# Grouped attention logits computed once and kept in SBUF, with GpSimd subtracting their maximum

## The chip, the cores and the metric

The kernel runs on one core of one Trainium2 chip. The time is the device time in microseconds of one execution. Five engines matter here: TensorE (PE) multiplies matrices into PSUM, VectorE (DVE), ScalarE (ACT) and GpSimd (POOL) work elementwise, and SyncE (SP) issues most of the loads. PSUM has eight banks of 128 partitions x 512 fp32; GpSimd has no operand in PSUM in this kernel.

## The reference, cut to what matters

Four cross-attention layers in fp32 run one after the other on x (4 batches, 512 queries, 256 channels) against one context (4 batches, 1024 keys, 512 channels). Layers 0, 2 and 3 are masked: 16 heads of 64.

```python
logits = einsum('bhqd,bhkd->bhqk', q, k) * scale + col_bias   # col_bias: a few key columns get -20*(1-mask)
probs  = softmax(logits)
out    = einsum('bhqk,bhkd->bhqd', probs, v) @ Wo + bo + residual
```

Layer 1 is grouped: an RMS norm of x, 16 query heads of 16 that share 4 key and value heads, no bias column, no `bo`:

```python
xn     = rmsnorm(x) * norm_w
scores = einsum('btgrd,bsgd->bgrts', qg, k) / 4      # 4 groups g, 4 query heads r in each
out    = einsum('bgrts,bsgd->btgrd', softmax(scores), v) @ wo + residual
```

## The kernel before

**Units and steps.** A unit (`Group`) is two masked heads of one layer and batch, or, in layer 1, the two kv groups of a half `h` (0 or 1) with one query head `r`. Logits are stored as keys x queries: block `t` of a unit is one tile of 128 keys by 2 x 512 queries, eight blocks in a unit, kept in slots `st[ring][t]` of SBUF. Two rings exist, each with eight blocks and a ninth slot (`mx`, also used as `acc`).

There are 96 masked units and 32 grouped ones. `order()` writes out 96 steps; each has one masked unit `g`, and 32 of them also have one grouped unit `lam`. The grouped units stand in four blocks of eight steps, one block for each batch. In step n, `g1` is the masked unit of step n-1, and `coming` is the grouped unit of step n+1. All engines execute the order in which the Python code issues the instructions (a manual schedule), and a semaphore holds an instruction back until its inputs and its output place are free.

**PSUM places.** `Place(width)` takes one or two banks, and always the ones that were given back longest ago, when the program is written; `back()` gives them back, and `late=` makes them look younger than they are. Which bank an instruction writes is therefore fixed in the program, and the matrix engine waits if the last reader of that bank has not finished.

**A masked unit.** `scores(g)`: eight pairs of matmuls into PSUM, ACT copies every block to SBUF (L674), DVE keeps a running maximum in the place of block 0 (L678). `max_quarters` (L715, L723, L747) and `max_everywhere` (L754) reduce it over the keys and spread it. DVE subtracts it (L759), ACT takes exponentials (L765), GpSimd adds the blocks (`running_sum`, L804) into `acc`. One step later `attend(g1)` (L694) multiplies with the values, `reciprocal_sums` (L820 to L834) and `scale_out` (L845) normalise, and after that `project_out` (L863) projects two units at a time and DVE adds the result to the state (L885).

**A grouped unit before.** Its heads have 16 dimensions in strips of 32 rows, so four matmuls run side by side in the array: `logits_pair(g, i)` (L643) makes two blocks at once. It is called twice for each unit. In step n-1 `maxima_pair` makes the logits for the maximum alone: DVE takes the maximum directly from PSUM (L635), and nothing is stored. `lower_queries` then writes minus the maximum into the query tile, into row 16 of every strip, where the keys hold a one (the bias `row16` in `k_grouped`, L503). In step n `exponentials_pair` makes the logits again, now already lowered, and ACT takes the exponentials from PSUM into SBUF (L651). The step's order on the matrix engine is: `scores(g)`, then four times two blocks of `attend(g1)` and one `logits_pair` of `lam`, then the fill.

**The fill.** After that come the rest of a step's matmuls, each 1.7 to 3.6 us in a planner's clock `now`: `project_out`, `project_q`, then keys of the next two units (L478, after odd masked units) or values (L519, after even ones), with the pairs of `coming` between them, and `attend(lam)`. DVE's subtractions and ACT's exponentials are issued between them by `events`, a list with due times in the same clock. A step in this text is called keys step or values step by its fill.

Of the kernel before, what the change touches and what calls it, by code (L numbers as in the profile page):

```python
# [28 lines left out]

# [48 lines left out]
def kernel(ctx: ExitStack, tc: tile.TileContext, a: dict, out: bass.AP):  # L78
# [18 lines left out]
    class Place:  # L97
        def __init__(self, width=2):
            free = given_back
            if width == 2:  # L100
# [19 lines left out]
    def st_slot(n):  # L120
# [11 lines left out]

    row16 = t_([P, 2], "row16", "row16")
    nc.vector.reduce_sum(
        row16[:, 0:1], ident.rearrange("p (g d) -> p g d", d=32)[:, :, 16], axis=AX.X
    )
    nc.vector.tensor_scalar(row16[:, 1:2], row16[:, 0:1], -1.0, None, ALU.mult)

# [346 lines left out]
    def k_grouped(g, h, part):  # L485

        if h == 0 and part == 0:
            g.kts = [t_([P, T // 2], f"kt1{i}", f"kt1{i}_{g.name}") for i in range(2)]
            g.kt = g.kts[0]
        if part == 0:  # L490
            g.k_place = Place(1)
        w = g.k_place
        m = w.ap
        for k in (2 * part, 2 * part + 1):
            for odd in range(2):
                nc.tensor.matmul(  # L496
                    m[64 * odd : 64 * (odd + 1), :], lhsT=g.w["k"][:, k, 64 * h : 64 * (h + 1)],
                    rhs=ctx_t[g.b][:, k, :].rearrange("p (i e q) -> p e i q", e=2, q=P)[:, odd],
                    start=(k == 0), stop=(k == KT - 1),
                )  # L500
        if part:
            return lambda: (
                nc.scalar.activation(g.kts[h], m, AF.Identity, bias=row16[:, 0:1]), w.back()  # L503
            )
# [124 lines left out]
    def maxima_pair(g, i):  # L629

        for odd, w in enumerate(logits_pair(g, i)):
            if i == 0 and odd == 0:
                nc.scalar.copy(g.mx, w.ap)  # L633
            else:
                nc.vector.tensor_tensor(g.mx, g.mx, w.ap, ALU.max)  # L635
            w.back()

    def logits_pair(g, i):
        ws = [Place(), Place()]
        for odd in range(2):  # L640
            for j in range(2):
                rows = slice(64 * odd + 32 * j, 64 * odd + 32 * (j + 1))
                nc.tensor.matmul(  # L643
                    ws[odd].ap[:, j * S : (j + 1) * S], lhsT=g.kt[rows, i * P : (i + 1) * P],
                    rhs=g.qt[rows, :], start=True, stop=True,
                )
        return ws

    def exponentials_pair(g, i):
        for odd, w in enumerate(logits_pair(g, i)):  # L650
            nc.scalar.activation(g.st[2 * i + odd], w.ap, AF.Exp)  # L651
            w.back()

    def scores(g):
# [3 lines left out]
        for t in range(NT):  # L658
# [16 lines left out]
            if t:  # L675
                w.back()
                top = g.mx_place.ap
                nc.vector.tensor_tensor(top, top, g.st[t], ALU.max)  # L678

    def place_out(g, width=1):  # L680
        g.place = Place(width)
        g.po, g.psum = g.place.ap[:, 0:S], g.place.ap[:, S:]
# [23 lines left out]
    def keep_odd(g):  # L706
        half = gq[g.b, "o"][64 * g.h : 64 * (g.h + 1), :]
        nc.vector.tensor_tensor(half, half, g.po[64:128, :], ALU.add)
        g.place.back()
# [16 lines left out]
    def lower_queries(g):  # L726


        half = max_halves(g, g.mx)
        every = t_([P, S // 32, 1], "every1", f"every1_{g.name}")  # L730
        for c in range(4):
            cols = slice(c % 2 * S // 32, (c % 2 + 1) * S // 32)
            nc.vector.tensor_tensor(
                every[32 * c : 32 * (c + 1), :, 0], half[0:32, cols], half[32:64, cols], ALU.max
            )

        m = g.mx[:, 0:S]
        nc.vector.transpose(
            m.rearrange("p (b r) -> p b r", r=32), every.to_broadcast([P, S // 32, 32])
        )  # L740
        nc.vector.scalar_tensor_tensor(g.qt, m, row16[:, 1:2], g.qt, ALU.mult, ALU.add)

# [8 lines left out]
    def max_everywhere(g):  # L751
        g.mb_place = Place()
        g.mb = g.mb_place.ap
# [4 lines left out]
    def subtract(g, t):  # L758
        nc.vector.tensor_tensor(g.st[t], g.st[t], g.mb, ALU.subtract)  # L759
        if t == NT - 1:  # L760
            g.mb_place.back()
# [82 lines left out]
    def scale_out(g):  # L844
        nc.vector.tensor_tensor(g.ot, g.po, g.ot, ALU.mult)  # L845
        g.place.back()

    def project_out(*of):
# [23 lines left out]
        def add():  # L872
# [13 lines left out]
            w.back()  # L886
# [56 lines left out]
    for b in range(B):  # L943
        first = next(g for g in masked if (g.b, g.l, g.u) == (b, 0, 0))
        for n, part_of in enumerate(load_parts(b, first.n == 0)):
            at_step = -1
            if first.n:
                before = masked[first.n - 2]
                at_step = step_of[before.l, before.b, before.u] - 5 + n
# [40 lines left out]
    turned = []  # L990
    left = {b: 32 - 4 for b in range(B)}

    for n in range(len(steps) + 2):
# [46 lines left out]
        pairs = []  # L1040
# [10 lines left out]
        def pair(i):  # L1051
            if i == 0:
                behind_exponentials()
            maxima_pair(coming, i)
            if i == NT // 2 - 1:
                lower_queries(coming)

        if coming:
            share(coming)
            coming.mx = st_slot((NT + 1) * (count % 2) + NT)  # L1060
        if lam:

            lam.st = [st_slot((NT + 1) * ((count if g else count + 1) % 2) + t) for t in range(NT)]
# [7 lines left out]


        if g:
            g.now = NT if masked_at(g.n + 1) else 4
            scores(g)

        ending = n >= len(steps) - 2
        if g1 and (g or lam):
            place_out(g1, 2 if ending else 1)
        if g:  # L1080
            max_quarters(g)
            if not lam:
                g.mx_place.back()
                max_everywhere(g)
        if turned or lam and g1:

            w = Place(1)
            if lam and g1:
                reciprocal_sums(g1, w.ap)
            for each in turned:  # L1090
                normalise_grouped(each, w.ap)
            w.back(late=12 if turned else 0)
        turned.clear()
        if lam:
            for i in range(NT // 2):
                if g1:
                    attend(g1, range(2 * i, 2 * i + 2))
                if coming and not g:
                    pair(i)
                exponentials_pair(lam, i)  # L1100
                if i == 0 and g:
                    g.mx_place.back()
                if not g:
                    if i == 1 and outs:
                        project_out(*outs.pop(0))()
                    if i == 2 and queries:
                        project_q(queries.pop(0))()
            if g and queries:


                project_q(queries.pop(0))()
            if g1:
                scale_out(g1)
                ready.append(g1)
            if g:
                max_everywhere(g)
        elif g1 and g:
# [3 lines left out]
        elif g1:  # L1121
            attend_last(g1)
            adds = [project_out(*each) for each in outs]
            outs = []
# [9 lines left out]
        if coming and (g or not lam):  # L1134
            pairs += [((12.0 if lam else 11.0 if g else 0.0) + 2.5 * i, i) for i in range(NT // 2)]

        fill, of_grouped = (
            [
                (1.8 * len(each), lambda each=each: project_out(*each))
                for each in outs if lam or each[0].masked == m
            ]
            for m in (True, False)
        )
        if lam:
            of_grouped = []
        outs = []  # L1150
        of_queries = [(1.7, lambda each=each: project_q(each)) for each in queries]
        fill += of_queries
        if lam:

            def attend_grouped():
                lam.v = head(lam).v
                place_out(lam)
                attend(lam)
                return lambda: keep_even(lam)

            fill.append((3.6, attend_grouped))
            late.append(lambda: keep_odd(lam))
# [18 lines left out]
        if follows and follows.l and follows.u == 0:  # L1181

            fill[-1:-1] = [(1.7, lambda: project_q(follows))]
        if g1 and g and ending:
# [9 lines left out]
        for us, w in fill:  # L1194
            while pairs and pairs[0][0] <= now:
                pair(pairs.pop(0)[1])
                now += 1.0
                pairs = [(max(at, now + 1.6), i) for at, i in pairs]
# [5 lines left out]
        while pairs:  # L1204
            pair(pairs.pop(0)[1])
# [36 lines left out]
```

## Time and profile before

| | |
|---|---|
| median of 3 runs | 3692.93 us (3689.32 to 3693.71) |
| the profiled execution | 3692.11 us; its span 3690.3 us |
| busy, share of the span | PE 99%, DVE 80%, ACT 57%, POOL 44% |
| granted TensorE clock | 0.999 |
| the four blocks of eight steps with a grouped unit, from one `scores` to the `scores` after the block | 372.74, 372.37, 372.34, 373.11 us |

The spans of the blocks are differences of the start times of the bias matmuls (L670) of their first steps. Durations in the profile are those of one execution; instructions of one engine overlap by their pipeline, so the distance from start to start can be a little shorter than a duration (ACT copies: 1051 ns each, eight in 7.43 us) or longer where each needs the one before (DVE maxima: 1233 ns each, seven in 9.25 us).

### The profile page before, as it was taken

Reading aid. Unit: us, or ns where it says so; the run is one execution under the profiler, and the core shown is the slowest. Engines: PE = TensorE matmul, PEld = TensorE weight load, DVE = VectorE, ACT = ScalarE, POOL = GpSimd, SP = SyncE. Lnnn points to the kernel's source line nnn. Section 1 sums busy time; section 2 is a strip of 40 time slices with the busy share of each in tenths; the row PEclk is TensorE's granted clock in tenths of the full one; section 3 lists DMA queues with packets and bytes.
Section 4 is the critical chain, followed back from the end, with each engine's and each line's share of the span. In section 5 each row is a group of like instructions: output and inputs, shape, how many; then the busy total and the mean of one; then the engine's idle time right before and its main releaser. Section 6 shows DMA issues by size and latency. Waiting matters only on the chain.

```text
span 3690.3 us, 42021 instructions
## 1 busy us (share of the span) xinstructions
PE 3656.6 (99%) x15534; PEld 1709.0 (46%) x15534; DVE 2970.3 (80%) x3912; ACT 2112.2 (57%) x2433; POOL 1622.7 (44%) x749
## 2 busy tenths in 40 slices
PE   8999999999999999999999999999999999999999
PEld 4554444444444444444545445454444445454454
DVE  7777788877888778887888778887788878888787
ACT  4555565555555656556555555555565565555554
POOL 3555433333333333333554545555333334545454
PEclk9999999999999999999999999999999999999999
DMA  2101100000000000000000110000100010000100
GB/s 65 43 32 40 34 28 22 21 21 23 22 22 21 21 23 22 22 22 18 26 18 26 49 38 26 26 26 18 33 22 22 13 33 18 26 26 26 32 28 9
DMA packets 137681, 98.16 MB, mean 27 GB/s; under 512 B 41720, under 2 KB 133368, under 8 KB 137476
## 3 DMA queue, kind: packets, MB, share of 16 engines
q1 hardware_dynamic: 131822, 82.37, 7.6%
q0 software_dynamic: 2560, 8.39, 0.8%
q10 hardware_dynamic: 3094, 4.72, 0.5%
q8 instruction: 122, 2.00, 0.2%
q14 instruction: 83, 0.68, 0.1%
HBM read 89.16 MB, written 2.10 MB: 25 GB/s over the span
## 4 chain that ended last, share of the span: by engine, by line
PE 94%; DVE 3%; ACT 1%; issue 1%; DMA 0%; POOL 0%; ACTq 0%; DVEq 0%; POOLq 0%
PE ps L694 21%; PE ps L519 18%; PE ps L478 18%; PE ps L664 17%; PE ps L643 8%; PE ps L863 5%; PE ps L575 5%; DVE ps L678 1%; DVE st L759 1%; PE ps L542 1%; PE ps L496 1%; PE ps L670 1%; ACT st L651 0%; PE ps L374 0%; ACT st L674 0%
## 5 line engine op out<-in xcount | busy, mean ns | idle before, releaser
L804 POOL TENSOR_TENSOR st<-st 128x1024 f32<-128x1024 f32 x668 | 1578.9, 2364 | 2014.0 <-ACT st L765 1969.2
L678 DVE TENSOR_TENSOR ps<-ps,st 128x1024 f32<-128x1024 f32 x672 | 828.4, 1233 | 430.4 <-ACT st L674 368.5
L765 ACT ACTIVATE st<-st 128x1024 f32<-128x1024 f32 x768 | 782.2, 1054 | 424.5 <-DVE st L759 412.6
L759 DVE TENSOR_TENSOR st<-st,ps 128x1024 f32<-128x1024 f32 x768 | 881.7, 1213 | 3.2
L694 PE MATMUL ps<-st,v 128*64 128x512 f32 (+1 forms) x4064 | 810.9, 598 | 0.0
L674 ACT COPY st<-ps 128x1024 f32<-128x1024 f32 x768 | 713.8, 1051 | 64.2 <-PE ps L670 63.0
L664 PE MATMUL ps<-qt,kt 64*128 64x512 f32 x3072 | 703.3, 597 | 0.9 <-ACT st L674 0.7
L478 PE MATMUL ps<-ctx,wk 128*128 128x512 f32 x1536 | 691.6, 601 | 2.2 <-ACT ctx L380 2.2
L519 PE MATMUL ps<-wv,ctx 128*128 128x256 f32 x3072 | 690.3, 382 | 0.0
L519 PEld LDWEIGHTS ps<-wv,ctx 128*128 128x128 f32 x3072 | 577.1, 190 | 152.5 <-issue 57.3
L694 PEld LDWEIGHTS ps<-st,v 128*64 128x64 f32 (+1 forms) x4064 | 231.2, 130 | 551.5 <-issue 467.4
L478 PEld LDWEIGHTS ps<-ctx,wk 128*128 128x128 f32 x1536 | 286.5, 191 | 395.3 <-issue 368.0
L664 PEld LDWEIGHTS ps<-qt,kt 64*128 64x128 f32 x3072 | 283.9, 186 | 358.0 <-ACT st L674 164.4
L635 DVE TENSOR_TENSOR st<-st,ps 128x1024 f32<-128x1024 f32 x224 | 273.5, 1221 | 151.8 <-ACT st L633 91.3
L651 ACT ACTIVATE st<-ps 128x1024 f32<-128x1024 f32 x256 | 248.1, 1021 | 154.7 <-PE ps L643 124.1
L643 PE MATMUL ps<-qt,kt 32*128 32x512 f32 x2048 | 305.4, 640 | 4.9 <-DVE st L759 3.4
L483 ACT COPY kt<-ps 128x512 f32<-128x512 f32 x192 | 111.4, 580 | 318.2 <-PE ps L478 318.0
L526 ACT COPY v<-ps 128x512 f32<-128x512 f32 x192 | 111.6, 583 | 248.2 <-PE ps L519 247.5
L581 ACT ACTIVATE qt<-ps 128x512 f32<-128x512 f32 x96 | 57.0, 594 | 269.1 <-PE ps L575 269.1
L575 PE MATMUL ps<-x,wq 128*128 128x512 f32 x384 | 188.8, 614 | 1.7 <-ACT x L352 1.1
L863 PE MATMUL ps<-ot,wo 128*128 128x512 f32 x384 | 176.5, 602 | 4.2 <-ACT st L651 3.5
L643 PEld LDWEIGHTS ps<-qt,kt 32*128 32x128 f32 x2048 | 90.2, 183 | 182.5 <-ACT st L651 51.9
(147 smaller groups left out, 1630.8 us busy)
## 6 DMA issues: line engine op xcount, KB each, us to landing
wk<-in_L_xattn_Wk_dram SPq DMA_DIRECT2D x47, 512.0 KB, 3.5
wv<-in_L_xattn_Wv_dram SPq DMA_DIRECT2D x47, 512.0 KB, 3.6
wq<-in_L_xattn_Wq_dram SPq DMA_DIRECT2D x96, 128.0 KB, 3.5
wo<-in_L_xattn_Wo_dram SPq DMA_DIRECT2D x96, 128.0 KB, 3.3
qt<-qt ACTq DMA_DIRECT2D x32, 128.0 KB, 2.2
xraw<-in_x_dram SPq DMA_DIRECT2D x3, 512.0 KB, 4.1
out_dram<-out SPq DMA_DIRECT2D x3, 512.0 KB, 3.7
wq<-in_L_xattn_wq_dram SPq DMA_DIRECT2D x32, 32.0 KB, 2.4
```

Source lines behind the costliest of these rows:

```text
L478: nc.tensor.matmul(m, lhsT=g.w["k"][:, k, :], rhs=ctx_t[g.b][:, k, n * 512 : (n + 1) * 512], start=(k == 0), stop=(k == KT - 1),)
L519: nc.tensor.matmul(m[:, half * 2 * P : (half + 1) * 2 * P], lhsT=ctx_t[g.b][:, k, t * P : (t + 1) * P], rhs=g.w["v2"][:, k, :], start=(k = ...
L575: nc.tensor.matmul(m, lhsT=g.wq[:, k, :], rhs=x[:, k, :], start=(k == 0), stop=(k == KC - 1))
L643: nc.tensor.matmul(ws[odd].ap[:, j * S : (j + 1) * S], lhsT=g.kt[rows, i * P : (i + 1) * P], rhs=g.qt[rows, :], start=True, stop=True,)
L664: nc.tensor.matmul(m[:, j * S : (j + 1) * S], lhsT=g.kt[g.rows[j], keys], rhs=g.qt[g.rows[j], :], start=True, stop=t > 0,)
L674: nc.scalar.copy(g.st[t], m)
L678: nc.vector.tensor_tensor(top, top, g.st[t], ALU.max)
L694: nc.tensor.matmul(g.po[at, :], lhsT=g.v[:, t, rows], rhs=g.st[t][:, j * S : (j + 1) * S], start=(t == first), stop=(t == last),)
L759: nc.vector.tensor_tensor(g.st[t], g.st[t], g.mb, ALU.subtract)
L765: nc.scalar.activation(st, st, AF.Exp)
L804: nc.gpsimd.tensor_tensor(g.acc, g.st[0] if t == 1 else g.acc, g.st[t], ALU.add)
L863: nc.tensor.matmul(m[:, k * S : (k + 1) * S], lhsT=each.wo[:, k * P : (k + 1) * P], rhs=each.ot, start=each is g, stop=each is of[-1],)
```

## The change

The logits of a grouped unit are made once, in its own step. `grouped_pair` makes two blocks, ACT copies both to SBUF, and DVE keeps a running maximum, as for a masked unit. The maximum is reduced and spread into a tile in SBUF (`mb`), GpSimd subtracts it from the eight blocks (`subtract_grouped`), and ACT takes the exponentials in place. `maxima_pair`, `lower_queries` and the row of ones are gone.

The order of a step with a grouped unit changes with it. First come the four rounds of `attend(g1)` and `grouped_pair(lam)`, then DVE's work for `lam` and `g1` (maximum, reciprocal sums, scaling, normalising of a grouped pair), the projections of queries, and only then `scores(g)`. The exponentials of `g`'s blocks 4 to 7 are not issued in their own step but carried into the next, two behind each `grouped_pair`. `attend(lam)` becomes the last item of the fill. Several `back(late=)` calls shift the choice of banks, and the context transposes of batches 0 and 2 are due two steps earlier.

```diff
-    def maxima_pair(g, i):
-        for odd, w in enumerate(logits_pair(g, i)):
-            if i == 0 and odd == 0:
-                nc.scalar.copy(g.mx, w.ap)
-            else:
-                nc.vector.tensor_tensor(g.mx, g.mx, w.ap, ALU.max)
-            w.back()
-    def exponentials_pair(g, i):
-        for odd, w in enumerate(logits_pair(g, i)):
-            nc.scalar.activation(g.st[2 * i + odd], w.ap, AF.Exp)
-            w.back()
+    def grouped_pair(g, i):
+        if i == 0:
+            g.mx_place = Place()
+        for odd in range(2):
...
+        for t in (2 * i, 2 * i + 1):
+            w = g.places[t]
+            nc.scalar.copy(g.st[t], w.ap)
+            if t:
+                w.back()
+                nc.vector.tensor_tensor(g.mx_place.ap, g.mx_place.ap, g.st[t], ALU.max)
+    def subtract_grouped(g, t):
+        nc.gpsimd.tensor_tensor(g.st[t], g.st[t], g.mb, ALU.subtract)
...
+        if lam:
+            share(lam)
+            lam.st = [st_slot((NT + 1) * (count % 2) + t) for t in range(NT)]
...
+            for i in range(NT // 2):
+                attend(g1, range(2 * i, 2 * i + 2))
+                grouped_pair(lam, i)
+                pass_carried(2)
+            max_quarters(lam)
+            lam.mx_place.back(late=5)
+            max_everywhere(lam)
+            for t in range(NT):
+                subtract_grouped(lam, t)
+            w = Place(1)
+            reciprocal_sums(g1, w.ap)
+            scale_out(g1)
+            for each in turned:
+                normalise_grouped(each, w.ap)
+            w.back(late=12)
...
+            run(of_queries)
...
         if g:
             g.now = NT if masked_at(g.n + 1) else 4
-            scores(g)
+            scores(g, pass_carried)
+        pass_carried(NT)
...
+        if lam:
+            for t in range(NT):
+                events.append((-3.0 + 2.36 * t, lambda t=t: nc.scalar.activation(lam.st[t], lam.st[t], AF.Exp)))
         if g:
             for t in range(NT):
-                events.append((0.7 + 1.2 * t, lambda t=t: subtract(g, t)))
-                events.append((3.3 + 1.22 * t, lambda t=t: exponentials(g, t)))
+                events.append(
+                    (3.7 + 0.01 * t if lam else 0.7 + 1.2 * t, lambda t=t: subtract(g, t, behind))
+                )
+                exp = lambda g=g, t=t: exponentials(g, t)
+                if not lam:
+                    events.append((3.3 + 1.22 * t, exp))
+                elif t < 4:
+                    events.append((14.5 + 1.22 * t, exp))
+                else:
+                    carried.append(exp)
```

More of the change, by code (lines that the diff above doesn't have):

```diff
@@ L97, with __init__ @@
     class Place:
-        def __init__(self, width=2):
+        def __init__(self, width=2, beside=None):
             free = given_back
-            if width == 2:
+            if beside and beside.banks[0] ^ 1 in free:
+                at = beside.banks[0] ^ 1
+            elif width == 2:
                 at = min(
@@ L131 @@
     nc.vector.memset(eps, EPS)
[L133 to L137, printed above, removed]
     def one_row(j):
@@ L501, in k_grouped @@
         if part:
-            return lambda: (
-                nc.scalar.activation(g.kts[h], m, AF.Identity, bias=row16[:, 0:1]), w.back()
-            )
+            return lambda: (nc.scalar.copy(g.kts[h], m), w.back())
     def v_pair(g, n, half):
@@ L626, in rms_norm @@
         return evacuate
[L629 to L639 removed]
+    def grouped_pair(g, i):
+        if i == 0:
+            g.mx_place = Place()
         for odd in range(2):
+            t = 2 * i + odd
+            w = Place() if t else g.mx_place
             for j in range(2):
@@ L643, in logits_pair, with scores @@
                 nc.tensor.matmul(
-                    ws[odd].ap[:, j * S : (j + 1) * S], lhsT=g.kt[rows, i * P : (i + 1) * P],
+                    w.ap[:, j * S : (j + 1) * S], lhsT=g.kt[rows, i * P : (i + 1) * P],
                     rhs=g.qt[rows, :], start=True, stop=True,
                 )
-        return ws
-    def exponentials_pair(g, i):
-        for odd, w in enumerate(logits_pair(g, i)):
-            nc.scalar.activation(g.st[2 * i + odd], w.ap, AF.Exp)
-            w.back()
-    def scores(g):
+            g.places.append(w)
+        for t in (2 * i, 2 * i + 1):
[6 more added lines that the diff above has]
+        nc.gpsimd.tensor_tensor(g.st[t], g.st[t], g.mb, ALU.subtract)
+    def scores(g, between):
         g.st = [st_slot((NT + 1) * g.ring + t) for t in range(NT)]
@@ L678, in scores, with place_out @@
                 nc.vector.tensor_tensor(top, top, g.st[t], ALU.max)
-    def place_out(g, width=1):
-        g.place = Place(width)
+            between()
+    def place_out(g, width=1, beside=None):
+        g.place = Place(width, beside)
         g.po, g.psum = g.place.ap[:, 0:S], g.place.ap[:, S:]
@@ L708, in keep_odd @@
         nc.vector.tensor_tensor(half, half, g.po[64:128, :], ALU.add)
-        g.place.back()
+        g.place.back(late=8)
     def over_quarter(out_, of, op):
@@ L724, in max_halves @@
         return half
[L726 to L741, printed above, removed]
     def max_quarters(g):
@@ L751, in max_everywhere @@
     def max_everywhere(g):
-        g.mb_place = Place()
-        g.mb = g.mb_place.ap
+        if g.masked:
+            g.mb_place = Place()
+            g.mb = g.mb_place.ap
+        else:
+            g.mb = t_([P, 2 * S], "stage", f"mb_{g.name}")
         nc.vector.transpose(
@@ L756, in max_everywhere, with subtract @@
         )
-    def subtract(g, t):
+    def subtract(g, t, late=0):
         nc.vector.tensor_tensor(g.st[t], g.st[t], g.mb, ALU.subtract)
         if t == NT - 1:
-            g.mb_place.back()
+            g.mb_place.back(late)
     def exponentials(g, t):
@@ L845, in scale_out, with project_out @@
         nc.vector.tensor_tensor(g.ot, g.po, g.ot, ALU.mult)
-        g.place.back()
-    def project_out(*of):
+        g.place.back(late=6)
+    def project_out(*of, late=0):
         g = of[0]
@@ L885, in add @@
                 nc.vector.tensor_tensor(acc, y, x if opens else acc, ALU.add)
-            w.back()
+            w.back(late)
         left[g.b] -= len(of)
@@ L948 @@
                 before = masked[first.n - 2]
-                at_step = step_of[before.l, before.b, before.u] - 5 + n
+                at_step = step_of[before.l, before.b, before.u] - (5 if b in (1, 3) else 7) + n
             parts.setdefault(at_step, []).append(part_of)
@@ L990 @@
     turned = []
+    carried = []
     left = {b: 32 - 4 for b in range(B)}
@@ L1039 @@
         late = []
-        pairs = []
         def pass_events(us):
@@ L1049, in behind_exponentials, with pass_carried @@
                 late.pop(0)()
[L1051 to L1063, printed above, removed]
+        def pass_carried(count=1):
+            for _ in range(count):
+                if carried:
+                    carried.pop(0)()
         queries = []
@@ L1070 @@
                 queries.append(each)
+        behind = 8 if lam else 0
+        of_outs = [
+            (1.8 * len(each), each[0].masked, lambda each=each: project_out(*each, late=behind))
+            for each in outs
+        ]
+        of_queries = [(1.7, lambda each=each: project_q(each)) for each in queries]
+        of_grouped = [(us, w) for us, of_masked, w in of_outs if not of_masked]
+        fill = [(us, w) for us, of_masked, w in of_outs if of_masked]
+        ending = n >= len(steps) - 2
+        if lam:
+            share(lam)
+            lam.st = [st_slot((NT + 1) * (count % 2) + t) for t in range(NT)]
+            lam.places = []
+            before = at(n - 1)[1]
+            place_out(g1, beside=before.place if before else None)
+            for i in range(NT // 2):
[13 more added lines that the diff above has]
+            w.back(late=12)
+            turned.clear()
+            ready.append(g1)
+            run(of_queries)
+            fill += of_grouped
+            of_queries = of_grouped = []
         if g:
             g.now = NT if masked_at(g.n + 1) else 4
-            scores(g)
-        ending = n >= len(steps) - 2
-        if g1 and (g or lam):
+            scores(g, pass_carried)
+        pass_carried(NT)
+        if g1 and g and not lam:
             place_out(g1, 2 if ending else 1)
@@ L1081 @@
             max_quarters(g)
[L1082 to L1085, printed above, removed]
+            g.mx_place.back()
+            max_everywhere(g)
+        if turned:
             w = Place(1)
-            if lam and g1:
-                reciprocal_sums(g1, w.ap)
             for each in turned:
                 normalise_grouped(each, w.ap)
[L1092 to L1117, printed above, removed]
+            w.back(late=12)
+            turned.clear()
+        fill += of_queries
+        if g1 and g and not lam:
             attend(g1)
@@ L1120 @@
                 late.append(lambda: normalise(g1))
-        elif g1:
+        elif g1 and not g:
             attend_last(g1)
-            adds = [project_out(*each) for each in outs]
-            outs = []
+            adds = [w() for _, w in fill + of_grouped]
+            fill, of_grouped = [], []
             reciprocal_rows(g1.ot, g1.psum, g1.mx)
@@ L1128 @@
                 add()
+        if lam:
+            for t in range(NT):
+                events.append((-3.0 + 2.36 * t, lambda t=t: nc.scalar.activation(lam.st[t], lam.st[t], AF.Exp)))
         if g:
             for t in range(NT):
-                events.append((0.7 + 1.2 * t, lambda t=t: subtract(g, t)))
-                events.append((3.3 + 1.22 * t, lambda t=t: exponentials(g, t)))
-            events.sort(key=lambda e: e[0])
[L1134 to L1162, printed above, removed]
+                events.append(
[6 more added lines that the diff above has]
+                    events.append((14.5 + 1.22 * t, exp))
+                else:
+                    carried.append(exp)
+            events.sort(key=lambda e: e[0])
         kk = masked[1:2] if n == 0 else masked[g.n + 1 : g.n + 3] if g and g.n % 2 else []
@@ L1183, with attend_grouped @@
             fill[-1:-1] = [(1.7, lambda: project_q(follows))]
+        if lam:
+            def attend_grouped():
+                lam.v = head(lam).v
+                place_out(lam)
+                attend(lam)
+                return lambda: keep_even(lam)
+            fill.append((3.6, attend_grouped))
+            late.append(lambda: keep_odd(lam))
         if g1 and g and ending:
@@ L1194 @@
         for us, w in fill:
[L1195 to L1198, printed above, removed]
+            if lam and w is attend_grouped:
+                pass_events(99.0)
             done = w()
@@ L1203 @@
                 done()
-        while pairs:
-            pair(pairs.pop(0)[1])
         behind_exponentials()
```

## The prediction

> **What bounds the kernel now.** I read the page's first and fourth parts, then the costliest groups, then the timelines of one step by engine.
>
> ```profile
> PE 3656.6 (99%) x15534; PEld 1709.0 (46%) x15534; DVE 2970.3 (80%) x3912; ACT 2112.2 (57%) x2433; POOL 1622.7 (44%) x749
> PE 94%; DVE 3%; ACT 1%; issue 1%; DMA 0%; POOL 0%; ACTq 0%; DVEq 0%; POOLq 0%
> ```
>
> The matrix engine is busy for 99% of the span and is 94% of the chain that ended last: nobody keeps it waiting, so a matmul removed is time gained, as long as no new wait replaces it. DVE's 80% is the second limit. The groups that the change touches or lengthens:
>
> ```profile
> L804 POOL TENSOR_TENSOR st<-st 128x1024 f32<-128x1024 f32 x668 | 1578.9, 2364 | 2014.0 <-ACT st L765 1969.2
> L651 ACT ACTIVATE st<-ps 128x1024 f32<-128x1024 f32 x256 | 248.1, 1021 | 154.7 <-PE ps L643 124.1
> L643 PE MATMUL ps<-qt,kt 32*128 32x512 f32 x2048 | 305.4, 640 | 4.9 <-DVE st L759 3.4
> L635 DVE TENSOR_TENSOR st<-st,ps 128x1024 f32<-128x1024 f32 x224 | 273.5, 1221 | 151.8 <-ACT st L633 91.3
> ```
>
> One keys step of the first block, in PE's timeline (start, length), from its first `attend` pair:
>
> ```profile
> 595.24 1.94 PE L694 MATMUL ps<-st,v 128*64 128x512 f32 x8
> 597.10 1.14 PE L643 MATMUL ps<-qt,kt 32*128 32x512 f32 x8
> 598.17 1.94 PE L694 MATMUL ps<-st,v 128*64 128x512 f32 x8
> ...
> 612.61 3.64 PE L694 MATMUL ps<-st,v 128*32 128x512 f32 x32
> 616.18 5.42 PE L478 MATMUL ps<-ctx,wk 128*128 128x512 f32 x12
> ```
>
> Two key blocks of `attend(g1)` take 1.86 us from start to start, a logits pair 1.07, `attend(lam)` 3.57, four key matmuls (eight of these records) 3.6. The other engines in the same timelines (the last two DVE rows are from the next step, with `normalise_grouped` between them):
>
> ```profile
> 589.34 7.43 ACT L674 COPY st<-ps 128x1024 f32<-128x1024 f32 x8 [0.69 <-PE ps L670]
> 591.30 9.25 DVE L678 TENSOR_TENSOR ps<-ps,st 128x1024 f32<-128x1024 f32 x7 [0.51 <-ACT st L674]
> 600.59 1.25 DVE L715 TRANSPOSE_TENSOR_REDUCE quarter<-ps 128x32 f32<-128x1024 f32 x1
> 602.85 1.24 DVE L715 TRANSPOSE_TENSOR_REDUCE ps<-st 128x32 f32<-128x1024 f32 x1
> 607.24 1.25 DVE L754 STREAM_TRANSPOSE ps<-every 128x1024 f32<-128x1024 f32 x1
> 612.04 17.04 POOL L804 TENSOR_TENSOR st<-st 128x1024 f32<-128x1024 f32 x7 [25.94 <-ACT st L765]
> 653.73 0.68 DVE L810 STREAM_TRANSPOSE ps<-o 128x512 f32<-128x512 f32 x1
> 656.11 0.68 DVE L845 TENSOR_TENSOR ot<-ps,ot 128x512 f32<-128x512 f32 x1
> ```
>
> From these: ACT copies every 0.91 us; seven chained maxima 9.3; maximum to quarters 2.26; reciprocal sums and scaling 4.39; a spread 1.28; normalising a grouped pair 2.38; GpSimd one sum every 2.44, the last 2.36. An answer crosses engines in about 0.1 us (pair ends 598.24, ACT starts 598.34).
>
> **What is removed.** Half of the logits pairs: 32 units x 4 x 1.07 = 137 us of PE. Nothing hid them, so 137 us is the most that can be won. `lower_queries` (3.8 us of DVE per unit) goes; the new quarters and spread (2.26 + 1.28) replace it, and the 224 maxima stay: DVE keeps its load, 306 us of busy time per block in the windows view, 38 per step.
>
> **What is added beside other work.** ACT: 256 copies and 256 exponentials in place of 32 and 256, 224 x 0.91 = 204 us, 6.4 per step on 27.8 (222 per block), so 34 us. GpSimd: 256 subtractions x 2.36 = 605 us; a step has 15 operations, 36.6 us. The spread goes to SBUF (L738 before wrote SBUF too: 0.71 us for half the size). All fit into a step of 46.6 us as work; the cost must come from order. No load is added on SP's queue; the context parts of two batches are issued two steps earlier, which I cost at nothing, since the DMA engines are 3 to 21% busy in the steps of and before the first block (if one came late, its transposes would hold PE by as much). The query copies that ACT issues for grouped units now stand between two copies of the same step, which DVE does not yet wait for.
>
> **What is moved, and the new waits.** A unit's slots are `g1`'s slots: copy t may not overwrite a block before GpSimd's sum t has read it, and sums 4 to 7 need exponentials that are now carried into this step, two behind each pair. Behind that copy on ACT stand all copies of `scores`; behind the maximum on DVE stand reciprocals, scaling and only then `g`'s maxima. The built program fixes the banks: in 28 of 32 steps the second key or value group of the fill writes the place of `g`'s own maximum, free only after DVE's reduction. So PE waits for DVE. Keys step, us from its first `attend`:
>
> - PE two blocks and a pair: 1.86 + 1.07 = 2.9.
> - ACT two copies, then exponential 4: 3.0 + 2 x 0.91 + 1.05 = 5.9.
> - GpSimd sums 4 to 7: 6.0 + 3 x 2.44 + 2.36 = 15.7.
> - ACT copy 7: 15.8 + 1.05 = 16.9.
> - DVE last maximum 1.3, quarters 2.26, spread 1.28, reciprocal and scaling 4.39: from 17.0 to 26.2. Seven maxima of `g` 9.3, reduction 1.25: 36.7.
> - PE three key groups 3 x 3.6 from 36.8, then `attend(lam)` 3.57: **51.2**.
>
> A values step normalises the grouped pair in the same DVE chain: +2.4, **53.6**. PE itself would be ready at 34.6 and 34.3: its first score waits for copy 7, scores then alternate with copies in two places (26.2 and 27.7), `project_out` waits for the last copy (31.0 and 30.7), then one group of 3.6. So it stands idle for 2.2 and 5.1 us. Covered: the eight subtractions end at 21.9 + 19.4 = 41.3, their last exponential at 42.4, five us before `attend(lam)`; were GpSimd that late, each us would count.
>
> The first step of a block carries nothing and normalises nothing: copy 7 at 13.8, and the held bank is only its last group; the subtractions decide, 18.8 + 19.4 + 1.1, then the last of `attend(lam)`: 44.1.
>
> **The sum.** A block: 44.1 + 4 x 51.2 + 3 x 53.6 = 409.7. The four were 1490.6 together: +148. The step before each block loses its four maxima pairs: -4 x 4.3 = -17. In the step after a block, four carried exponentials stand between the copies of `scores`, which have one spare place: about 2.1 us per block instead of 0.91 for four blocks, +5 each; nearest rows give 0 (hidden) to 7.4 (eight more ACT slots): +20, bounds 0 to 30. Together +151 on the profiled execution's 3692.1 (0.8 below the median): 3843, on the median **3844**.
>
> **A gap and the clock.** The profile shows cold matmuls only at the start, after waits for loads, against the same form later:
>
> ```profile
> 9.01 3.78 PE L575 MATMUL ps<-x,wq 128*128 128x512 f32 x4 [1.10 <-ACT x L352]
> 654.50 1.98 PE L575 MATMUL ps<-x,wq 128*128 128x512 f32 x4
> ```
>
> Four records cost 1.8 us more. Twelve values steps with a gap of 5 us could pay that each: 0 to +22. I take 0 into the sum, since gaps of 1 us inside the span before show no such stretch, and keep 22 for the range. [...]
>
> **Rivals.**
>
> 1. *The banks come back in time, and PE's saving counts.* Place: copy 7 and the reduction that frees `g`'s place. For it: every engine's work per step (DVE 38, ACT 34, GpSimd 36.6, PE 42.6, which is 372.4 less seven units' 4.28 and 1.7 of idle, over eight) is below the 46.6 us of a step before. It decides where a step gets under 46.6: the reduction at 32 instead of 36.7, and copy 7 at 14.5 instead of 16.9. Then 3692 - 137 + 20 = **3575**, floor 3555. Against it: the rows that make 36.7 are start-to-start distances, and the waits are in the built program.
> 2. *DVE does not hold the bank.* If only PE's own path counts (34.6 + 10.8 + 3.6 = 49.0; 48.8), a block is 44.1 + 4 x 49.0 + 3 x 48.8 = 386.5, +55 in all: 3692 + 55 - 17 + 20 = **3750**. It needs DVE five us faster than its rows.
> 3. *GpSimd or the clock cost more.* Subtractions at 3.0 us instead of 2.36 also lengthen the sums beside them: four x 0.64 in 28 steps, +72: **3915**. All 668 sums took 2.34 to 2.40 us beside a busy DVE, which speaks against it.
>
> That the change does not do what it says is out: the built program has 512 logits matmuls of grouped units instead of 1024.
>
> **Numbers.** My forecast 3844 (3790 to 3895) has 0.54, rival 1 0.16, rival 2 0.18, rival 3 0.12. The range takes in rival 2 and some of the way to rival 1, whose partial gains lie between, and most of rival 3: 3670 to 3905, leaving out about 0.14 below and 0.06 above. 0.2% is 7 us, about what a measurement can tell (three runs lay within 4.4). Faster 0.17, same 0.02, slower 0.81.
>
> **What would show it.** Right: PE waiting for DVE's quarter reduction before the second key group (about 2 us) or value group (about 5 us), 28 times; blocks near 410 us; copy 7 waiting for GpSimd, PE busy for about 3520 us. Wrong: blocks under 373 us, or PE's idle time behind ACT or behind the exponentials of `lam` instead.

## The result: 7.7% slower

| | before | after |
|---|---|---|
| median | 3691.25 us (3689.32 to 3693.71, 4 runs) | 3972.68 us (3972.0 to 3978.04, 4 runs) |
| ratio | | 1.0765, interval 1.0752 to 1.0777 |
| the profiled execution, its span | 3692.11, 3690.3 us | 3978.04, 3976.3 us |
| granted TensorE clock | 0.999 | 0.982 |

The direction was forecast, the size was not: 281 us more instead of 151, and 3973 lies above the range of 3670 to 3905. The page of the changed kernel, first the busy times, then the chain that ended last, then groups (busy us, mean ns of one, idle time before them and what ended it; PE's counts are of records, two for each matmul):

```profile
PE 3688.7 (93%) x14510; PEld 1678.0 (42%) x14510; DVE 3055.0 (77%) x3878; ACT 2338.3 (59%) x2657; POOL 2216.6 (56%) x1005
PE 69%; ACT 11%; DVE 10%; POOL 6%; issue 3%; ACTq 0%; DMA 0%; DVEq 0%; POOLq 0%; SPq 0%
L656 PE MATMUL ps<-qt,kt 64*128 64x512 f32 x3072 | 828.9, 643 | 142.4 <-ACT st L666 127.9
L631 PE MATMUL ps<-qt,kt 32*128 32x512 f32 x1024 | 190.2, 640 | 6.5 <-ACT st L638 6.5
L644 POOL TENSOR_TENSOR st<-st,mb 128x1024 f32<-128x1024 f32 x256 | 594.5, 2360 | 274.8 <-DVE mb L733 231.0
```

The halved logits are real: 1024 records and 190.2 us of busy time where there were 2048 and 305.4. PE was 94% of the chain and is 69%: nearly all of the other 31% is work of ScalarE, VectorE and GpSimd that the end waits for. PE's busy time did not fall to 3520 us, it rose to 3689. The row of `scores` (L656, before L664) says most of why: the same 3072 records took 828.9 us instead of 703.3. The list of PE's waits (total us, times, longest) names the new waits:

```profile
PE ps L656 <- ACT st L666: 127.9, 282, 2.2
PE ps L511 <- DVE quarter L708: 46.5, 12, 4.5
PE ps L842 <- ACT st L666: 27.9, 25, 1.2
PE ps L567 <- ACT st L638: 26.9, 29, 1.3
PE ps L656 <- ACT st L638: 13.4, 22, 1.3
PE ps L472 <- DVE quarter L708: 10.2, 10, 2.0
```

The forecast wait for DVE's quarter reduction is there (rows 2 and 6), 22 times and 57 us in all. The largest is another: `scores` waiting for ScalarE's copies, 282 times. Where the 286 us of span went, each stretch taken from the start of PE's first matmul in it (`attend` where a block of the changed kernel starts, `scores` elsewhere), with the prediction's own cuts:

| stretch | forecast | measured |
|---|---|---|
| four blocks (1490.6 before) | +148 | 1676.1, +185.5 |
| the step before each block, four | -17 | -26.6 |
| the step after each block, four | +20 | +32.4 |
| the 55 other steps, plain | 0 | +94.0 |

They add up to +285.3; the rest lies at the ends of the run. The steps before the blocks lost more than their four pairs because PE had also waited 0.95 to 1.35 us at these pairs, and the first pair had taken 2.1 to 2.5 us instead of 1.1.

A plain step, `scores` in PE's timeline (start, length, and in brackets the wait), first before, then after:

```profile
1937.56 6.17 PE L664 MATMUL ps<-qt,kt 64*128 64x512 f32 x28
```
```profile
2070.67 1.88 PE L656 MATMUL ps<-qt,kt 64*128 64x512 f32 x8
2072.91 2.05 PE L656 MATMUL ps<-qt,kt 64*128 64x512 f32 x8 [0.36 <-ACT st L666]
2075.21 2.05 PE L656 MATMUL ps<-qt,kt 64*128 64x512 f32 x8 [0.25 <-ACT st L666]
2077.51 1.13 PE L656 MATMUL ps<-qt,kt 64*128 64x512 f32 x4 [0.25 <-ACT st L666]
```

Before, 28 records run through. After, PE stops behind every second block until the copy of two blocks earlier is done: some 1.78 us more (1.6 to 1.9) in 47 of the 55 steps. No work was added to these steps. What the diff does change in them is one word, `late=6` in `scale_out`, by which the place that `attend` gives back looks young; in the built program the scores of a plain step then rotate over two pairs of banks, where before they rotated over three.

A values step and a keys step of the first block, the fill:

```profile
588.13 3.62 PE L511 MATMUL ps<-wv,ctx 128*128 128x256 f32 x16
595.35 12.16 PE L511 MATMUL ps<-wv,ctx 128*128 128x256 f32 x48 [3.60 <-DVE quarter L708]
...
643.78 3.60 PE L472 MATMUL ps<-ctx,wk 128*128 128x512 f32 x8
648.08 10.57 PE L472 MATMUL ps<-ctx,wk 128*128 128x512 f32 x24 [0.70 <-DVE quarter L708]
```

This is the wait that was forecast, before the second group, and its three groups follow (the last two rows are from the keys step). The steps run 54.8 and 51.1 us here (forecast 53.6 and 51.2).

### The profile page after: what moved, and what is told of

Same layout as the page of the kernel before. It is cut to its first block, busy times and chain, and to the rows that moved or that the text cites. A ratio compares the mean times of both kernels' runs of the same rounds, so it can differ in the third digit from the quotient of the medians.

```text
span 3976.3 us, 40262 instructions
## 1 busy us (share of the span) xinstructions
PE 3688.7 (93%) x14510; PEld 1678.0 (42%) x14510; DVE 3055.0 (77%) x3878; ACT 2338.3 (59%) x2657; POOL 2216.6 (56%) x1005
## 4 chain that ended last, share of the span: by engine, by line
PE 69%; ACT 11%; DVE 10%; POOL 6%; issue 3%; ACTq 0%; DMA 0%; DVEq 0%; POOLq 0%; SPq 0%
PE ps L511 17%; PE ps L472 16%; PE ps L687 15%; PE ps L656 10%; ACT st L666 8%; POOL st L783 6%; DVE ps L670 4%; PE ps L842 4%; PE ps L567 4%; ACT st L638 2%; DVE quarter L708 1%; PE ps L631 1%; ACT st L744 1%; PE ps L534 1%; PE ps L490 1%
## 5 line engine op out<-in xcount | busy, mean ns | idle before, releaser
L670 DVE TENSOR_TENSOR ps<-ps,st 128x1024 f32<-128x1024 f32 x672 | 828.2, 1232 | 452.5 <-ACT st L666 392.0
L656 PE MATMUL ps<-qt,kt 64*128 64x512 f32 x3072 | 828.9, 643 | 142.4 <-ACT st L666 127.9
L744 ACT ACTIVATE st<-st 128x1024 f32<-128x1024 f32 x768 | 772.8, 1055 | 261.2 <-DVE st L738 254.0
L738 DVE TENSOR_TENSOR st<-st,ps 128x1024 f32<-128x1024 f32 x768 | 879.2, 1213 | 2.2
L666 ACT COPY st<-ps 128x1024 f32<-128x1024 f32 x768 | 743.2, 1015 | 228.4 <-PE ps L656 168.4
L644 POOL TENSOR_TENSOR st<-st,mb 128x1024 f32<-128x1024 f32 x256 | 594.5, 2360 | 274.8 <-DVE mb L733 231.0
L511 PE MATMUL ps<-wv,ctx 128*128 128x256 f32 x3072 | 699.0, 389 | 46.5 <-DVE quarter L708 46.5
L472 PE MATMUL ps<-ctx,wk 128*128 128x512 f32 x1536 | 674.4, 595 | 12.5 <-DVE quarter L708 10.2
L511 PEld LDWEIGHTS ps<-wv,ctx 128*128 128x128 f32 x3072 | 599.6, 196 | 162.0 <-DVE quarter L708 51.3
L656 PEld LDWEIGHTS ps<-qt,kt 64*128 64x128 f32 x3072 | 261.4, 191 | 660.2 <-ACT st L666 485.9
L641 DVE TENSOR_TENSOR ps<-ps,st 128x1024 f32<-128x1024 f32 x224 | 276.1, 1233 | 278.8 <-ACT st L638 271.7
L638 ACT COPY st<-ps 128x1024 f32<-128x1024 f32 x256 | 249.7, 1021 | 154.8 <-PE ps L631 86.6
L1113 ACT ACTIVATE st<-st 128x1024 f32<-128x1024 f32 x256 | 256.9, 1053 | 15.6 <-POOL st L644 15.5
L567 PE MATMUL ps<-x,wq 128*128 128x512 f32 x384 | 190.2, 618 | 28.6 <-ACT st L638 26.9
L631 PE MATMUL ps<-qt,kt 32*128 32x512 f32 x1024 | 190.2, 640 | 6.5 <-ACT st L638 6.5
```

The source lines that it names most:

```text
L472: nc.tensor.matmul(m, lhsT=g.w["k"][:, k, :], rhs=ctx_t[g.b][:, k, n * 512 : (n + 1) * 512], start=(k == 0), stop=(k == KT - 1),)
L511: nc.tensor.matmul(m[:, half * 2 * P : (half + 1) * 2 * P], lhsT=ctx_t[g.b][:, k, t * P : (t + 1) * P], rhs=g.w["v2"][:, k, :], start=(k = ...
L567: nc.tensor.matmul(m, lhsT=g.wq[:, k, :], rhs=x[:, k, :], start=(k == 0), stop=(k == KC - 1))
L638: nc.scalar.copy(g.st[t], w.ap)
L644: nc.gpsimd.tensor_tensor(g.st[t], g.st[t], g.mb, ALU.subtract)
L656: nc.tensor.matmul(m[:, j * S : (j + 1) * S], lhsT=g.kt[g.rows[j], keys], rhs=g.qt[g.rows[j], :], start=True, stop=t > 0,)
```

## The experiments

Theory A: banks. Two choices of `back(late=)` set the time: `scale_out`'s in the plain steps, and the place of `g`'s maximum in the blocks, behind the chain from GpSimd's sums to DVE's reduction. The rivals put the time into clock, GpSimd's subtractions or the carried exponentials.

**1. `late=6` only in steps with a grouped unit.**

```diff
-    def scale_out(g):
+    def scale_out(g, late=0):
-        g.place.back(late=6)
+        g.place.back(late=late)
-            scale_out(g1)
+            scale_out(g1, late=6)      # in steps with a grouped unit
```

> The changed kernel, but scale_out gives its bank back with late=6 only in steps with a grouped unit, with 0 in plain steps. In the traces 52 plain steps take about 1.78 us more after the change, 94 us in all, and in the program the scores of those steps write two pairs of banks in turn where they wrote three. Theory A (the returned bank that is made to look young takes one pair away from scores): plain steps go back to 30.02 and 33.38 us and the time falls by about 94 us, to 3880; steps with a grouped unit stay within 1 us of 51 and 54. Theory B (the plain steps are longer for another reason, such as GpSimd's or DVE's longer queues behind the blocks): within 10 us of 3973.

Measured: 3873.8 us, ratio 1.0495 (1.0477 to 1.0512): 99 us less than the changed kernel. The plain steps together take 1774.9 us again (before 1773.3, after 1867.3).

**2. The same word put into the kernel before**, in its plain steps (`normalise`), and nothing else of the change.

```diff
-        scale_out(g)
+        scale_out(g, late=6)           # in normalise
```

> The kernel before, with one edit: normalise, which is called in plain steps alone, lets scale_out give the bank back with late=6. The scores of plain steps then write two pairs in turn. Theory A: about 58 plain steps lengthen by 1.8 us, 3691 + 100 = 3790, and ScalarE's copies show as what PE waits for in scores. Theory B: the kernel stays within 0.3% of 3691.

Measured: 3786.48 us, 1.0261 (1.0244 to 1.0278): 96 us more, at a clock of 0.999. Its timeline of `scores` shows the stop of the changed kernel:

```profile
1964.72 1.88 PE L664 MATMUL ps<-qt,kt 64*128 64x512 f32 x8
1966.96 2.05 PE L664 MATMUL ps<-qt,kt 64*128 64x512 f32 x8 [0.36 <-ACT st L674]
```

Taken out it gives 99 us, put in it costs 96. A third of the loss has nothing to do with grouped logits.

**3. The place of `g`'s maximum looks younger**, so that only the last of the fill's four groups writes its banks.

```diff
-            g.mx_place.back()
+            g.mx_place.back(late=4 if lam else 0)
```

> The changed kernel, but in steps with a grouped unit the place of the masked unit's maximum is given back with late=4, so that the second and third group of the fill go to other banks and only the last group writes that place. Theory A (the timetable: PE waits there for DVE's reduction): a keys step falls from 51.2 to 49.0 and a values step from 53.6 to 48.8, 28 steps, about -90 us, 3880; the wait of L472 and L511 for the quarter reduction (57 us on PE) is gone. Theory C (DVE's chain only shows there, and the next wait takes its place): less than 30 us won, with the time gone to waits for the exponentials of the grouped unit before its attend, or for copies.

Measured: 3891.72 us, 1.054 (1.0523 to 1.0558): 81 us less than after. Both waits for the quarter reduction are gone from PE's list. The values steps fell from 55.2 to 49.3 us as a mean, near PE's own path of the prediction (48.8). The keys steps hardly fell, from 51.9 to 51.4, where 49.0 was expected: single ones take up to 56 us. So nearly all of the gain lies in the values steps, where the changed kernel waits 46.5 us and then runs 21 us slower (see the clock below).

**4. GpSimd's sums of blocks 4 to 7 left out** in steps with a grouped unit, so that nothing holds copies 4 to 7.

```diff
-            g.now = NT if masked_at(g.n + 1) else 4
+            g.now = NT if masked_at(g.n + 1) and not lam else 4
```

> The changed kernel, with GpSimd's sums of blocks 4 to 7 left out in steps with a grouped unit (the denominators there lack these blocks). Theory A (the copies of the grouped logits wait for those sums, and the chain from copy 7 sets the step): copy 7 ends 2.5 us earlier in 28 steps, about -70 us, 3900. Theory D (ScalarE's own row of copies and exponentials is as long): copy 7 stays, within 15 us of 3973.

Measured: 3931.25 us, 1.0648 (1.0631 to 1.0666): 41 us less, some 60% of what was expected. DVE's timeline in a values step, the last maxima of `lam` after, then in this run:

```profile
570.67 1.23 DVE L641 TENSOR_TENSOR ps<-ps,st 128x1024 f32<-128x1024 f32 x1 [0.31 <-ACT st L638]
573.10 1.23 DVE L641 TENSOR_TENSOR ps<-ps,st 128x1024 f32<-128x1024 f32 x1 [1.20 <-ACT st L638]
574.37 1.25 DVE L708 TRANSPOSE_TENSOR_REDUCE quarter<-ps 128x32 f32<-128x1024 f32 x1
```
```profile
563.77 5.25 DVE L641 TENSOR_TENSOR ps<-ps,st 128x1024 f32<-128x1024 f32 x4 [1.15 <-ACT st L638]
569.05 1.25 DVE L708 TRANSPOSE_TENSOR_REDUCE quarter<-ps 128x32 f32<-128x1024 f32 x1
```

The first grouped logits of these steps start at 558.08 and 554.07. The reduction follows after 16.29 us and after 14.98: only 1.3 us earlier. After the change the last maxima wait for copies, in this run the last four run back to back, so DVE's own chain is the next limit. The 41 us, too, are 1.5 us for each of the 28 steps, as a mean. GpSimd's sums do hold the step, but there was only about that much to be had behind them.

**5. The subtractions left out**, and DVE's minus-maximum unused.

```diff
-            for t in range(NT):
-                subtract_grouped(lam, t)
-                events.append((-3.0 + 2.36 * t, lambda t=t: nc.scalar.activation(lam.st[t], lam.st[t], AF.Exp)))
+                events.append((-3.0 + 2.36 * t, lambda t=t: nc.scalar.activation(lam.st[t], lam.st[t], AF.Exp, scale=0.05)))
```

> The changed kernel with GpSimd's 256 subtractions left out (the grouped exponentials are of logits scaled by 0.05 and not lowered, so that they stay finite). Theory A (the subtractions end five us before they are needed and lie off the path): within 40 us of 3973, what is won coming only from the first steps of blocks and from DVE instructions that GpSimd slows. Theory E (605 us of added GpSimd work is what the change costs): at least half of the 282 us comes back, 3830 or less.

Measured: 3972.93 us, 1.076 (1.0744 to 1.0777): no difference. GpSimd's 595 us are wholly covered. The run showed something else. Two small DVE operations, by groups (busy us, mean ns), after, then in this run:

```profile
L723 DVE TENSOR_TENSOR every<-half 32x32 f32<-32x32 f32 x512 | 134.9, 264 | 17.7
L716 DVE TENSOR_TENSOR half<-quarter 64x32 f32<-64x32 f32 x128 | 67.6, 528 | 4.4
```
```profile
L723 DVE TENSOR_TENSOR every<-half 32x32 f32<-32x32 f32 x512 | 93.2, 182 | 17.7
L716 DVE TENSOR_TENSOR half<-quarter 64x32 f32<-64x32 f32 x128 | 24.0, 187 | 4.4
```

They were slower beside the subtractions, by 85 us in total, and that too was covered.

**6. Six of the eight exponentials in their own step**, two carried.

```diff
-                elif t < 4:
+                elif t < 6:
```

> The changed kernel, but six instead of four of the masked unit's exponentials are issued in their own step and two are carried, so that only sums 6 and 7 wait for the front of the next step. Theory A: copy 7 ends at about 14 instead of 17 us after the first attend, DVE's chain and the bank follow, 28 x 3.0 = -84 us, 3890. Theory D (ScalarE is as full there): the two exponentials block ScalarE before attend of the grouped unit, and the time stays within 15 us of 3973.

Measured: 3931.34 us, 1.0648 (1.0632 to 1.0665): 41 us less, half of what was expected and as much as in experiment 4. That is the limit found there: from the third step of a block on, the reduction of `lam` begins 16.6 us after the step's first `attend`, where it was 18.15 after the change and 16.85 in experiment 4.

**7. Four edits together.**

```diff
     # experiment 1, experiment 3, and
-            lam.mx_place.back(late=5)
+            lam.mx_place.back(late=2)
-                elif t < 4:
+                elif t < 6 or not at(n + 1)[1]:
```

> The changed kernel with four edits together: late=6 of scale_out only in grouped steps, the masked maximum's place given back with late=4, the grouped maximum's place with late=2 instead of 5 (scores then use it as a second pair at once), and six exponentials in their own step (all eight if no grouped step follows). By the timetable a keys step is 45.8 us and a values step 45.6, against 47.2 before: blocks 364 instead of 372.6, the four steps before blocks 17 us less: about 3640. Rival: the halved clock and waits of scores for ScalarE's copies remain, 2 us per grouped step: 3690 to 3710, no gain over the kernel before.

Measured: 3773.01 us (5 runs), 1.022 (1.0206 to 1.0234): the fastest form of the change that was run, and still 81 us behind the kernel before. Both forecasts were too low. Its plain steps are as before (1775.4 us); the 40 steps of the blocks and their neighbours take 1915.7 us against 1836.9. The step after a block even became longer (53.6 us in two of the four, 49.7 after the change), though nothing is carried into it: the exponentials now stand in front of its copies, and PE waits up to 5.3 us for them. PE's longest waits:

```profile
PE ps L656 <- ACT st L666: 59.0, 105, 5.3
PE ps L567 <- ACT st L638: 33.7, 29, 1.4
PE ps L842 <- ACT st L666: 32.8, 28, 1.5
PE ps L656 <- DVE quarter L708: 23.6, 20, 1.4
PE ps L631 <- ACT st L638: 15.4, 28, 1.4
PE ps L656 <- ACT st L638: 11.6, 18, 1.3
```

These add up to 176 us, more than the 137 us of matmuls that the change removes. They are no longer one wait: five of the six rows stand behind ScalarE's copies for the two kinds of scores.

**8 to 10. No `late` at all.** If the plain steps lose by `late`, what do the steps with a grouped unit gain by it? Run 8 takes every `late=` out, run 9 adds experiment 3's edit to it, run 10 experiment 6's to that.

```diff
-        g.place.back(late=8)           # place of lam; and late=6, 5, 12, 12
+        g.place.back()
-        behind = 8 if lam else 0
+        behind = 0
     # runs 9 and 10:
-            g.mx_place.back()
+            g.mx_place.back(late=4 if lam else 0)
     # run 10:
-                elif t < 4:
+                elif t < 6:
```

> The changed kernel with every back(late=) taken as back(): the order of work is the change's, the banks are those given back longest ago. In the built program scores then rotate over three pairs of banks in plain steps and in steps with a grouped unit, and the maximum's place of g is written by the third group of keys or values instead of the second. Theory A (banks): the plain steps win their 94 us back; in a step with a grouped unit only two key groups, not three, follow the reduction, so 28 steps lose some 3.6 us: 3973 - 94 - 100 = 3780, and the waits for the quarter reduction become shorter. Theory B (the ring gates): the steps with a grouped unit wait for copy 7 and its chain whatever the banks are, only the plain steps win: 3875 to 3880.

> As the run without any late=, and in addition the place of g's maximum looks four returns younger in steps with a grouped unit, so that the fill's four groups use four other banks. Theory A: what is left is PE's own path, 49.0 us for a step minus some 2.3 us for scores that now have three pairs of banks, and no wait for the quarter reduction: 28 steps x (52.2 - 46.7) = 154 and the 94 of the plain steps: 3725, range 3690 to 3760, so still not below the kernel before, because the projections and scores wait for copy 7 behind GpSimd's sums. Theory B: a new wait of PE takes the place (attend(lam) behind the exponentials of lam, or the first scores behind DVE), and it lands at 3770 as the run with four edits did.

> As the run before it, and six of the eight exponentials of g are issued in their own step, so that only two are carried. Theory A (copy 7 waits for sums 4 to 7, whose exponentials are carried): the copies come 1 to 2 us earlier in 28 steps and the step after a block has two exponentials less between its copies, 30 to 60 us less than the run with four carried: 3670 to 3700, about the time of the kernel before. Theory B: sums 1 to 5 now lie behind DVE's subtractions of g late in the step, as in the run with four edits, and nothing or little is won: within 15 us of the run with four carried.

Measured: 3937.63 us, 1.0662 (1.0646 to 1.0678); 4014.17 us, 1.087 (1.0855 to 1.0885); 3965.48 us, 1.0743 (1.0728 to 1.0758). The two theories on record for the first two runs both fell; of the third, only the difference of 49 us to its neighbour came as theory A had it. The edit of experiment 3, worth 81 us on the changed kernel, costs 77 us between runs 8 and 9. The plain steps are back (1773.6, 1773.8, 1773.8 us), so the steps with a grouped unit have become slower than the change left them (the clock granted in the profiled executions is 0.963, 0.963 and 0.965). PE's timeline of a values step in run 9:

```profile
567.68 1.13 PE L656 MATMUL ps<-qt,kt 64*128 64x512 f32 x4
576.90 7.25 PE L656 MATMUL ps<-qt,kt 64*128 64x512 f32 x24 [8.09 <-DVE o L795]
584.57 1.98 PE L842 MATMUL ps<-o,wo 128*128 128x512 f32 x4 [0.41 <-ACT st L666]
586.39 14.21 PE L511 MATMUL ps<-wv,ctx 128*128 128x256 f32 x64
602.56 5.51 PE L687 MATMUL ps<-st,v 128*32 128x512 f32 x40 [1.96 <-DVE st L738]
```

The waits for the quarter reduction are gone from the fill, and `scores` run through once they run, but its third pair waits 8.09 us for DVE's normalising, whose place it now writes: the place that `late=12` kept out of reach. And `attend(lam)` waits for DVE's subtractions of `g`, 47.7 us in all in run 9. One shift cost 94 us in the plain steps; together, the shifts are what keeps `scores` out of DVE's chain in the others. Which of them does how much of that was not tried one by one.

## Why the prediction was wrong in size

- **The plain steps** are the step that failed. The prediction's list of what is moved looked at banks only where a grouped unit stands, and the sum gave 0 to 55 steps that the diff reaches by one shared function. Experiments 1 and 2 show +94 to +99 us for that alone. The order of banks in the program would have shown it: those of a plain step's scores were there to be read as those of the fill were.
- **The timetable of a block's step** held in its mechanism. In the step that starts at 1012.1, copy 7 ended 17.3 us after the start (16.9 forecast), `g`'s maxima began at 26.6 (26.2), and the reduction ended at 37.1 (36.7); in this step PE came later still, by the clock (0.50 granted from 1028.6 to 1042.2). PE waited for the reduction 22 times, not 28, and for 57 us, where idle times of 2.2 and 5.1 us had made 96. Experiment 3 shows that the bank under `g`'s maximum is what makes DVE's chain count (81 us, where rival 2 differs from the forecast by 94).
- **The blocks** came to +185.5 instead of +148. Of the missing 37, 19 lie in the values steps (55.2 us as a mean, 53.6 worked out), 11 in the keys steps, two of which took 55.3 and 56.5 us where PE was late by the clock (0.50 granted for 10.2 and 13.7 us in them), and 7 in the first steps (45.6 to 47.2 where 44.1 was worked out).
- **The clock** was mis-sized: 0 in the sum, with 22 kept for the range. The waits of the values groups were 2.0 to 4.5 us long, and the three groups behind each took 12.1 to 13.7 us where three times 3.6 is 10.8: over the twelve steps 21 us. All twelve paid: within 2.3 us of the end of each of these waits a stretch of 3.41 or 6.83 us begins in which the granted clock is 0.50. A further loss of clock came at gaps of one microsecond (0.50 granted over the 10 us from 1030, last section), which the prediction had passed over because it saw slow matmuls (3.78 us for four records) only at the start of the profile before. One stretch stands later in that profile, in the step before the fourth block: behind a wait of 1.35 us, four records of keys take 3.51 us instead of 1.98, and the granted clock is 0.50 for 3.41 us.

```profile
2643.31 2.49 PE L643 MATMUL ps<-qt,kt 32*128 32x512 f32 x8 [1.35 <-DVE st L759]
2645.73 3.51 PE L478 MATMUL ps<-ctx,wk 128*128 128x512 f32 x4
```

- **The step after a block** cost some 9 us, not 5, in three of four: its `scores` took 16.4 us instead of 7.3, between the copies and the carried exponentials as forecast, but with 0.50 of the clock granted for 10.24 us of it. By the order in which banks are handed out, blocks 1 to 4 of these three `scores` all write the same two banks; in the step that cost 5 us, only two blocks in a row do, and in runs 8 and 9, where `scores` have three pairs in turn, the step costs 3.7 us.

```profile
877.67 1.42 PE L656 MATMUL ps<-qt,kt 64*128 64x512 f32 x4 [2.16 <-ACT st L666]
880.25 2.08 PE L656 MATMUL ps<-qt,kt 64*128 64x512 f32 x4 [1.16 <-ACT st L666]
883.50 6.23 PE L656 MATMUL ps<-qt,kt 64*128 64x512 f32 x16 [1.17 <-ACT st L666]
```

- **The covered subtractions** and the sums behind them: the cover held (experiment 5). The slack of 1.3 to 1.5 us between GpSimd's and DVE's chains was not seen; the prediction named only the later of the two.
- **Rival 1** (3575) fell as argued: no run came under 3692. **Rival 2** (3750) is what experiment 7 comes nearest to, by other edits than it meant. **Rival 3**'s price by slower subtractions is refuted (2360 ns each); its clock half is real.

What stays open is how much of the blocks' excess the clock brings about. PE was busy for 122 of the 143 us with a granted clock of 0.50 (last section), so the slower matmuls alone come to some 61 us of the 286, an estimate that takes them at half speed (four records took 2.08 us there instead of 1.13); how the waits would fall at full clock no run shows, since none keeps the clock up and the waits in place. A third set of slots in SBUF, which would free the copies from GpSimd's sums, was not tried.

## What to carry to other kernels

A line of a diff is priced in every step that executes it, also in those the change is not about: here a default inside a shared helper cost a third of the loss. Where buffers are handed out in order of age, read the whole rotation of the built program before and after, in each kind of step; taking a buffer away from one user hands it to another, and taking a delay away can bring back a longer wait that it hid. And when work removed from the bounding engine is replaced by stages that other engines must pass on, ask for the second-latest chain as well as the latest: it is the most that mending the first can bring.

## What the hardware showed that was not expected

**The granted clock fell to 0.50 at gaps of one microsecond.** In the step from 1012.1, PE's timeline and the windows view (PE, PEld, DVE, ACT and POOL busy, then the granted clock):

```profile
1032.61 2.08 PE L656 MATMUL ps<-qt,kt 64*128 64x512 f32 x4 [1.11 <-ACT st L666]
1035.80 2.08 PE L656 MATMUL ps<-qt,kt 64*128 64x512 f32 x4 [1.11 <-ACT st L666]
...
1030.00:1040.00 10.00, 6.66 (x14) 1.51 (x12) 9.23 (x21) 3.32 (x4) 5.50 (x3) 0.50 0.00 0
```

Four records take 2.08 us instead of 1.13, PE is busy for two thirds of the time, no gap is longer than 1.3 us, and the granted clock is 0.50 over the whole 10 us. The clock record of this trace has 27 such stretches within the run, 143 us in all, each 3.41 us long or a multiple of it. In the 3.41 us ahead of each, PE was busy for 62% or less, in 23 of them for under half; nine had no gap over 1.35 us ahead of them. In the run cut into slices of 3.41 us, none with PE busy for under half was followed by full clock; 16 with 50 to 62% were, so the busy share alone does not tell the two apart. Each stretch ended only behind 3.41 us with PE busy for 86% or more, which pair, copy, pair, copy does not reach (65% in the rows above). Over the whole run the mean clock fell from 0.999 to 0.982.

**Small DVE operations beside GpSimd.** `half` and `every` take 0.19 and 0.18 us alone, and up to 1.80 and 2.28 us beside a subtraction: all 32 of `half` that run beside one take 1.27 us or more, all 96 others 0.19. Without the subtractions the longest is 0.19 (experiment 5). DVE's maxima, which have one operand in PSUM, stay at 1232 ns, and GpSimd's operation at 2360.
